# Where the band matmuls of the layer 0 attention get their queries: GpSimd copies, or zero-filled versions in scratch

## The chip, the cores and the metric

The kernel runs on one core of a Trainium2 chip. The core has a matrix engine (TensorE, PE in the profile; its weight loads are listed as PEld), a vector engine (VectorE, DVE), an engine for activations (ScalarE, ACT), a slower general engine (GpSimd, POOL) and a queue from which all transfers of this kernel are issued (SyncE, SP). Every engine works through its own list of instructions in order; an instruction that waits holds up all that stand behind it on that engine. The metric is the device time of one execution in microseconds (us); before the change it is 3945.27 us, the median of three runs (3943.41 to 3945.44).

## What is computed

A network of two layers in the macaron form works on x of 16 batches x 512 tokens x 128 features. Layer 0 is half a feed-forward block with 4-bit block quantization, attention with relative positions, and half a feed-forward block again; layer 1 has two mixture-of-experts blocks with a linear attention between them. The change touches only the attention of layer 0:

```
x = x + 0.5 * _L0_ffn_ref(_layernorm(x), ...)
x = x + _L0_attn_ref(_layernorm(x), ...)          # B=16, S=512, 16 heads of 8
x = x + 0.5 * _L0_ffn_ref(_layernorm(x), ...)
...
dist = jnp.clip(idx[None, :] - idx[:, None], -R, R) + R        # R = 64
pe_k = rel_emb_k[dist]; pe_v = rel_emb_v[dist]
q = q / sqrt(hd)
score = einsum('bhqd,bhkd->bhqk', q, k) + einsum('bhqd,qkd->bhqk', q, pe_k)
attn = softmax(score)
ctx = einsum('bhqk,bhkd->bhqd', attn, v) + einsum('bhqk,qkd->bhqd', attn, pe_v)
```

The second term of the score depends on the distance of query and key only within 64 tokens; outside it is constant per query. So it needs extra matmuls only for tiles near the diagonal, the band.

## The kernel before

**Units of work.** Layer 0 takes the 16 batches one after the other, each in two halves of 256 queries; batch b and half give unit u = 2b + half, 32 units in all. For a unit, `maxima` computes all scores once to find each query's maximum (VectorE, line 324), and `main` computes them a second time, with the negative maximum as an extra row of the contraction, takes exp on ScalarE (line 352) and multiplies by V (lines 361 and 363) and by the relative value table (line 378). Each pass has 32 tiles: 4 blocks of 128 keys by 8 blocks of 32 queries.

**A score tile** (`scores`) is 128 keys x 512 columns (8 values x, 16 heads, 4 residues j). Query 4x+j in the stored order of a block stands for one query; j is called its residue of four. Four matmuls (line 253) of 128 columns give q.k, with queries from `BD`, a tensor that is zero outside its diagonal blocks. If the tile is in the band, eight more matmuls (line 257) of 64 columns add the relative term: the table `ET`, shifted by x, is the stationary operand, and the queries of one x come from `TQ`. The 128 rows of the contraction are four groups of 32 partitions, one per residue; of each 24 rows are used (8 of the high half of the query, 8 of the low half, 8 of the high half again, f16 each). A column of residue j must be zero in the groups of the other residues. There are 8192 matmuls of line 253 and 7168 of line 257.

**How queries get there.** `prep` makes the queries of a batch: a projection on TensorE, a copy to SBUF on ScalarE that sorts them by block, x and j (line 276), the high half on VectorE and the low half on GpSimd (`f16split`, lines 142 and 143). SP writes them to scratch in device memory, QS[16 heads, 29 rows, 512] (line 282), and writes four more rows for the side terms (line 289). `load` reads them back for one half: into `BD` (line 309), and into `TS` (line 310), each residue group receiving all 256 queries. Then four GpSimd copies (line 313), one per residue, take every fourth query from TS and put it into TQ[64 blocks of four, 16 heads, 4 residues], whose other entries were set to zero once in the setup. So the 64 columns of a line 257 matmul lie side by side in TQ. There are three TQ and three BD, used in turn by unit, and one TS.

**Order.** The program is one stream of generators that `interleave` steps through by due times: `main` of unit u, the maxima of the following unit, `prep` of a batch two ahead (in the first 0.7 of an even unit), the feed-forward block of other batches in small steps, and `fin`, the end of the attention. `load` of unit u+1 is issued in the middle of the maxima of unit u. The scheduler then simulates this stream and fixes the order on each engine. All transfers are in the SP queue: the writes of the queries, the loads of BD, TS and KS, the maxima's way through scratch (MD, lines 336 and 338: written, read back into row 28 of BD; `main` needs it), the value part's way (RD, lines 387 and 390), loads and stores of x (lines 456 and 467).

**Other work on VectorE and GpSimd.** The feed-forward block quantizes on both: for a tile of 128 x 704 or 128 x 256, VectorE lines 70 to 78 (74, 76, 77 and 78 read and write SBUF only), then GpSimd lines 79 and 81. The layer norm takes `ln_ve` on VectorE (line 58), a power on GpSimd (line 59) and `ln_mr` on VectorE (line 60).

Of the kernel before, what the change touches and what calls it, by code (L numbers as in the profile page):

```python
# [9 lines left out]
F16 = mybir.dt.float16  # L10
# [130 lines left out]
def f16split(nc, src, hi, lo, eng_lo):  # L141
    nc.vector.tensor_copy(hi,src)
    eng_lo.tensor_tensor(lo,src,hi,ALU.subtract)

class Attn0:

    def __init__(a, s, wk, pp, wqkv, bqkv, wout, bout, rek, rev):
        nc=s.nc; a.s=s; a.nc=nc
        c=s.const; dr=s.dram
# [32 lines left out]
        lo=OFF+24-64  # L182
# [28 lines left out]
            nc.scalar.copy(a.TV[:,:,i*8:i*8+8,:].rearrange("p x v d -> p v x d"),ps.rearrange("p (v x d) -> p v x d",x=8,d=8))  # L211

        a.BD=[c.tile([128,4,4,256],F16,name=f"a0_BD{i}") for i in range(3)]
        a.TQ=[c.tile([128,64,16,4],F16,name=f"a0_TQ{i}") for i in range(3)]
        a.TS=c.tile([128,16,256],F16,name="a0_TS")
        a.KS=[c.tile([128,2,2048],F16,name=f"a0_KS{i}") for i in range(2)]
        a.V=[c.tile([128,4,2,168],F32,name=f"a0_V{i}") for i in range(2)]
        a.cr=[c.tile([128,1024],F32,name=f"a0_cr{i}") for i in range(1)]
# [12 lines left out]
            for sd in range(2): nc.scalar.activation(t[:,sd,:],a.BD[2].rearrange("p g h q -> p (g h q)")[:,0:2048],AF.Identity,bias=rm[:,sd:sd+1])  # L231
        zr=wk.tile([16,512],F16,name="zr"); nc.vector.memset(zr,0.0)
        a.QS=[dr.tile([16,29,512],F16,name=f"QS{i}") for i in range(2)]
        a.KSd=[dr.tile([16,24,512],F16,name=f"KSd{i}") for i in range(2)]
        a.MD=[dr.tile([16,256],F16,name=f"MD{i}") for i in range(2)]
        a.X=4*8*1024+1024
# [10 lines left out]
    def scores(a, out, kt, half, b, BD, TQ, KS):  # L247

        nc=a.nc; blk=half*8+b
        sd=a.side(kt,blk); ib=a.inband(kt,blk)  # L250
        o4=out.rearrange("p (x g c) -> p g x c",x=8,g=4)
        for g in range(4):
            nc.tensor.matmul(o4[:,g],KS[:,sd,g*512+kt*128:g*512+(kt+1)*128],BD[:,g,:,b*32:b*32+32].rearrange("p h (x j) -> p x h j",j=4),start=(g==0),stop=(not ib and g==3),skip_group_check=True)  # L253
        if ib:
            for x in range(8):
                w0=kt*128-blk*32-x+a.OFF
                nc.tensor.matmul(out[:,x*64:x*64+64],a.ET[:,w0:w0+128],TQ[:,b*8+x].rearrange("p h j -> p (h j)"),start=False,stop=(x==7),skip_group_check=True)  # L257

    xnT={}; pend={}; last=None
    def prep(a, b, xb, wk, pM):  # L260
        s=a.s; nc=a.nc
        i=b%2
        QS=a.QS[i]; KSd=a.KSd[i]
        xn=wk.tile([128,4,128],F32,name="xn")
        yield from s.ln_steps(xb,xn,wk,4)
        ps=pM.tile([128,512],F32,name="mps")
        for j in range(4): nc.tensor.transpose(ps[:,j*128:(j+1)*128],xn[:,j,:],a.ident)
        xnT=a.xnT[b]=wk.tile([128,512],F32,name="xnT",bufs=2); nc.scalar.copy(xnT,ps); yield
        for z in range(2):
            ps=pM.tile([128,512],F32,name="mps")  # L270
            nc.tensor.matmul(ps,a.w[:,z*128:(z+1)*128],xnT,start=True,stop=True)
            f=wk.tile([128,512],F32,name="qk0") if z==0 else wk.tile([128,4,128],F32,name="xn").rearrange("p a b -> p (a b)")
            if z==0:
                for hf in range(2):
                    c=slice(hf*256,hf*256+256)
                    nc.scalar.activation(f[:,c].rearrange("p (b x j) -> p b j x",j=4,x=8),ps[:,c].rearrange("p (b j x) -> p b j x",j=4,x=8),AF.Identity,bias=a.bq[:,0:1],scale=float(1/np.sqrt(8.0)))
                q=f
            else: nc.scalar.activation(f,ps,AF.Identity,bias=a.bq[:,1:2])
            hi=wk.tile([128,512],F16,name="qkhi",bufs=2); lo=wk.tile([128,512],F16,name="qklo")
            f16split(nc,f,hi,lo,nc.gpsimd)  # L280
            for p,t in enumerate((hi,lo,hi) if z==0 else (hi,hi,lo)):
                nc.sync.dma_start((QS,KSd)[z][:,p*8:p*8+8,:],t)
            yield
        ps=pM.tile([128,512],F32,name="mps")
        nc.tensor.matmul(ps[:32],a.eb.rearrange("p a b -> p (a b)"),q,start=True,stop=True)
        rhi=wk.tile([128,512],F16,name="qkhi",bufs=2)[:32]; rlo=wk.tile([128,512],F16,name="qklo")[:32]
        nc.vector.tensor_copy(rhi,ps[:32]); nc.vector.tensor_tensor(rlo,ps[:32],rhi,ALU.subtract)
        for sd in range(2):
            nc.sync.dma_start(QS[:,24+2*sd,:],rhi[16*sd:16*sd+16]); nc.sync.dma_start(QS[:,25+2*sd,:],rlo[16*sd:16*sd+16])
        yield  # L290
# [14 lines left out]
    def load(a, b, half):  # L305
        nc=a.nc; i=b%2
        u=(2*b+half)%3; BD=a.BD[u]; TQ=a.TQ[u]; QS=a.QS[i]
        for j in range(4):
            nc.sync.dma_start(BD[j*32:j*32+29,:,j,:],QS.rearrange("(g j) r q -> j r g q",j=4)[j][:,:,half*256:half*256+256])
            nc.sync.dma_start(a.TS[j*32:j*32+24],QS[:,0:24,half*256:half*256+256].rearrange("h r q -> r h q"))  # L310
        for j in range(4):
            p=slice(j*32,j*32+24)
            nc.gpsimd.tensor_copy(TQ[p,:,:,j],a.TS[p,:,j::4].rearrange("p h y -> p y h"))  # L313

    def maxima(a, b, half, wk, pS, pM):

# [121 lines left out]
def layer0(tc, s, w, src, dst, nb=16):  # L438
# [3 lines left out]
    with ExitStack() as c:  # L442
# [51 lines left out]
        def run(g):  # L494
            for _ in g: pass
        run(prep(0)); run(prepV(0)); loads(0); run(mxs(0,0)); loads(1); ffn2(head,1); run(prep(1)); run(part(14)); ffn2(head,2)
        S=[(part(99999),33*2*nb,W['part'],2*nb+W['part'])]
        for b in range(nb):
            for h in range(2):
                u=2*b+h  # L500
                def at(g,n,f,t): S.append((g,n,u+f,u+t))
                at(A.main(b,h,X,wk,big,pS,pA,pM),59,0,1)
                at(A.fin(b,h,X,wk,pM),5,1+W['fin'][0],1+W['fin'][1])
                at(tail(b,h),21,1+W['fin'][1]+.001,1+W['fin'][1]+W['tail'])
                if b+hl<nb: at(head(b+hl,h),21,*W['head'])
                if h==0 and b+pl<nb: at(prep(b+pl),11,*W['prep'])
                if h==1 and b+1<nb: at(prepV(b+1),1,*W['V'])
# [470 lines left out]
```

## Time and profile before

| what | value | from |
|---|---|---|
| median of 3 runs | 3945.27 us | the times |
| the profiled execution | 3944.92 us, of it a span of 3943.2 us | the times, the page |
| score tiles of layer 0 | first reduce at 117.6 us, last exp ends at 2083.5 us | rows of lines 324 and 352 |
| busy in 32 stretches of 61 us from 150 us on, mean | PE 53.98, DVE 46.24, ACT 29.24, POOL 21.33 us | busy time by stretch |
| DVE in two neighbouring stretches (943 to 1004, 1004 to 1065) | 53.05 and 42.30 us | the same |
| granted clock of TensorE in most of these stretches | 0.94 | the same |

Times in a row of the timeline are the start, from the start of the span, and the duration. A group's row in the page gives its count, its busy time, the mean duration of one, and how long the engine sat idle just ahead of it and who ended that. Matmuls are pipelined, so the rate of a matmul is read from the starts of neighbouring rows and not from its duration. Some 125 us pass from one batch to the next: the writes of the queries begin at 828.1, 952.3 and 1077.8 us.

### The profile page before, as it was taken

To read this page: it belongs to the slowest core of one execution; us is meant where nothing else is said; L and a number is where in the kernel's file an instruction comes from. 1 tells how busy PE (TensorE), PEld (TensorE's weight loads), DVE (VectorE), ACT (ScalarE), POOL (GpSimd) and SP (SyncE) were. 2 spreads that over 40 slices of the span, in tenths; PEclk is the share of its full clock that TensorE was granted. 3 is DMA by queue.
4 is the path that set the end of the run, shared out by engine and by line. 5 is a ranking of instruction groups with operands and counts; after the bars stand their busy time and mean duration, and the time that the engine had idled before them with its cause. 6 is when DMAs were issued, how large, how long until landed. Compare 5 with 4: busy or idle time off the path is not lost.

```text
span 3943.2 us, 98508 instructions
## 1 busy us (share of the span) xinstructions
PE 2997.4 (76%) x41613; PEld 2162.8 (55%) x41613; DVE 2588.3 (66%) x6567; ACT 1711.1 (43%) x3389; POOL 1100.2 (28%) x883
## 2 busy tenths in 40 slices
PE   4788898988889889899985577770688888888540
PEld 2566677676777667767763344430465555555320
DVE  5768777887778777887754366664546556555375
ACT  2245445444444445445442344531445445444321
POOL 4443433334233333433312011103311111010214
PEclk7799999999999999999996777875899899888665
DMA  1221222122121221112101100003321122111114
GB/s 51 48 53 40 55 44 50 42 47 54 43 48 35 56 50 40 49 39 56 40 19 45 42 25 33 30 22 88 92 71 53 48 68 65 44 52 29 58 33 122
DMA packets 263248, 194.88 MB, mean 49 GB/s; under 512 B 74428, under 2 KB 228886, under 8 KB 262679
## 3 DMA queue, kind: packets, MB, share of 16 engines
q1 hardware_dynamic: 262806, 188.59, 18.6%
q8 instruction: 327, 5.36, 0.6%
q14 instruction: 115, 0.93, 0.1%
HBM read 111.57 MB, written 76.92 MB: 48 GB/s over the span
## 4 chain that ended last, share of the span: by engine, by line
PE 42%; DVE 20%; DMA 10%; ACT 7%; POOL 2%; issue 2%; SPq 1%; DVEq 0%; POOLq 0%; ACTq 0%
PE sps L253 8%; PE mps L685 5%; PE sps L257 3%; DVE mx L324 3%; PE av L361 2%; PE pp L849 2%; PE rps L378 2%; DMA d_m<-FMD 2%; ACT f_PT L644 2%; PE av L363 1%; PE mps L649 1%; PE mps L138 1%; DVE moe L687 1%; DVE cx L403 1%; DMA X<-d_x 1%
## 5 line engine op out<-in xcount | busy, mean ns | idle before, releaser
L253 PE MATMUL sps<-a_BD,a_KS 128*128 128x128 f16 x8192 | 763.4, 225 | 162.6 <-DVE mx L324 117.4
L324 DVE TRANSPOSE_TENSOR_REDUCE mx<-sps 128x16 f32<-128x512 f32 x1024 | 708.3, 705 | 242.5 <-PE sps L253 140.0
L352 ACT ACTIVATE PT<-sps 128x512 f32<-128x512 f32 x1024 | 579.3, 597 | 512.6 <-PE sps L257 269.9
L253 PEld LDWEIGHTS <-a_KS 128*128 128x128 f16 x8192 | 548.9, 100 | 317.6 <-issue 267.1
L687 DVE SCALAR_TENSOR_TENSOR moe<-mps,oh,moe 128x128 f32<-128x128 f32 x1024 | 331.0, 345 | 240.6 <-PE mps L685 224.6
L79 POOL TENSOR_TENSOR q_M<-q_y,q_M 128x256 f32<-128x256 f32 (+2 forms) x135 | 158.1, 1172 | 795.2 <-DVE q_y L78 508.4
L59 POOL TENSOR_TENSOR ln_rs<-ln_ve,negh 128x4 f32<-128x4 f32 (+1 forms) x192 | 175.4, 922 | 720.2 <-DVE ln_ve L58 651.9
L257 PE MATMUL sps<-a_TQ,a_ET 128*128 128x64 f16 x7168 | 371.7, 195 | 3.2 <-POOL a_TQ L313 3.2
L313 POOL COPY a_TQ<-a_TS 24x1024 f16<-24x1024 f16 x128 | 330.4, 2581 | 93.8 <-PE sps L257 47.3
L257 PEld LDWEIGHTS <-a_ET 128*128 128x128 f16 x7168 | 311.0, 100 | 14.0 <-issue 12.2
L685 PE MATMUL mps<-f_W,T 128*128 128x512 f32 x512 | 288.1, 680 | 2.6 <-DVE moe L687 2.0
L361 PE MATMUL av<-PT,a_V 128*32 128x256 f32 (+2 forms) x3584 | 264.0, 346 | 0.0
L851 DVE TENSOR_TENSOR a_at<-pp,a_cm 128x1024 f32<-128x1024 f32 x128 | 154.5, 1219 | 90.3 <-PE pp L849 89.8
L378 PE MATMUL rps<-PT,a_TV 128*32 128x64 f32 x7168 | 212.3, 230 | 0.8 <-issue 0.6
L849 PE MATMUL pp<-a_F 64*128 64x128 f32 x2048 | 174.0, 309 | 17.5 <-DVE a_at L851 11.0
L849 PEld LDWEIGHTS pp<-a_F 64*128 64x128 f32 x2048 | 146.2, 209 | 63.8 <-issue 28.5
L378 PEld LDWEIGHTS rps<-PT,a_TV 128*32 128x32 f32 x7168 | 137.7, 112 | 60.4 <-issue 27.8
L649 PE MATMUL mps<-f_PT,v 128*32 128x128 f32 x1024 | 55.7, 388 | 149.8 <-ACT f_PT L644 149.8
L361 PEld LDWEIGHTS av<-PT,a_V 128*32 128x32 f32 x3584 | 130.5, 109 | 53.9 <-issue 15.1
L831 ACT ACTIVATE a_F<-pp 128x1024 f32<-128x1024 f32 x128 | 127.8, 1025 | 63.6 <-PE pp L829 54.8
L62 ACT ACTIVATE d_m<-d_m,ln_mr,ln_rs 128x128 f32<-128x128 f32 x128 | 52.2, 483 | 229.0 <-DVE ln_mr L60 173.9
L685 PEld LDWEIGHTS mps<-f_W,T 128*128 128x128 f32 x512 | 98.3, 214 | 90.6 <-issue 64.6
(320 smaller groups left out, 5657.1 us busy)
## 6 DMA issues: line engine op xcount, KB each, us to landing
a_TS<-QS SPq DMA_DIRECT2D x128, 192.0 KB
RD<-RV SPq DMA_DIRECT2D x32, 512.0 KB
a_KS<-KSd SPq DMA_DIRECT2D x128, 96.0 KB
a_QK<-a1d SPq DMA_DIRECT2D x128, 96.0 KB
xn<-X SPq DMA_DIRECT2D x32, 256.0 KB
YD<-xn SPq DMA_DIRECT2D x32, 256.0 KB
FMD<-moe SPq DMA_DIRECT2D x32, 256.0 KB
d_x<-X SPq DMA_DIRECT2D x32, 256.0 KB
```

The source lines that it names most:

```text
L59: nc.gpsimd.tensor_tensor(rs,ve,s.negh[:,:n],ALU.pow); yield
L79: nc.gpsimd.tensor_tensor(M[:P],y[:P],M[:P],ALU.subtract)
L253: nc.tensor.matmul(o4[:,g],KS[:,sd,g*512+kt*128:g*512+(kt+1)*128],BD[:,g,:,b*32:b*32+32].rearrange("p h (x j) -> p x h j",j=4),start=(g==0 ...
L257: nc.tensor.matmul(out[:,x*64:x*64+64],a.ET[:,w0:w0+128],TQ[:,b*8+x].rearrange("p h j -> p (h j)"),start=False,stop=(x==7),skip_group_chec ...
L313: nc.gpsimd.tensor_copy(TQ[p,:,:,j],a.TS[p,:,j::4].rearrange("p h y -> p y h"))
L324: r=nc.vector.tensor_reduce(mx[:,kt,:,bb],ps.rearrange("p (i c) -> p i c",c=32),axis=AX.X,op=ALU.max,apply_transpose=True)
L352: nc.scalar.activation(pt[:,:,bb*32:bb*32+32].rearrange("p h (x j) -> p x h j",j=4),ps.rearrange("p (x h j) -> p x h j",x=8,j=4),AF.Exp)
L361: nc.tensor.matmul(o[:,0:q3],V[:,kt,0,h*9:h*9+32],pt[:,h,0:q3],start=fs,stop=(kt==3),skip_group_check=True,tile_position=(0,cg*32))
L378: nc.tensor.matmul(rps[cg*32:cg*32+32,col:col+64],a.TV[:,x,v0:v0+4,:].rearrange("p v d -> p (v d)"), PT[k][:,:,bb*32+4*x:bb*32+4*x+4], sta ...
L685: nc.tensor.matmul(ps,yT[:,j*128:(j+1)*128],a.W[:,e2*4:e2*4+4,:],start=True,stop=True)
L687: nc.vector.scalar_tensor_tensor(moe[:,j,:],ps[:,e*128:(e+1)*128],oh[:,j,e2*4+e:e2*4+e+1],moe[:,j,:],ALU.mult,ALU.add)
L849: nc.tensor.matmul(ps[:,hh,bs],f[hh*64:hh*64+64,1,bs],f[hh*64:hh*64+64,0,bs],start=True,stop=True)
```

## The change

TS and the GpSimd copies go. In `prep`, after the split, the high half is copied once more by VectorE and the low half once more by GpSimd, into `HM`, two tiles of [128, 4, 512] that were set to zero in the setup: position [j, n] receives query n if n has residue j, and stays zero otherwise. SP writes each of the four versions to a new scratch tensor QM[4 residues, 16 heads, 24 rows, 512], three times (rows 0 to 7 high, 8 to 15 low, 16 to 23 high): 12 writes per batch of 128 partitions x 1 KB. In `load`, residue group j of TQ is filled straight from QM[j] by a transfer of the shape that TS had. TQ is now [128, 16 heads, 256 queries], and a line 257 matmul reads its 64 columns as 16 runs of 4 queries, one run per head.

```
-        a.TQ=[c.tile([128,64,16,4],F16,name=f"a0_TQ{i}") for i in range(3)]
-        a.TS=c.tile([128,16,256],F16,name="a0_TS")
+        a.TQ=[c.tile([128,16,256],F16,name=f"a0_TQ{i}") for i in range(3)]
+        a.HM=[c.tile([128,4,512],F16,name=f"a0_HM{i}") for i in range(2)]
+        for t in a.HM: nc.gpsimd.memset(t,0.0)
...
+        a.QM=[dr.tile([4,16,24,512],F16,name=f"QM{i}") for i in range(2)]
...
-                nc.tensor.matmul(out[:,x*64:x*64+64],a.ET[:,w0:w0+128],TQ[:,b*8+x].rearrange("p h j -> p (h j)"),start=False,stop=(x==7),skip_group_check=True)
+                nc.tensor.matmul(out[:,x*64:x*64+64],a.ET[:,w0:w0+128],TQ[:,:,b*32+4*x:b*32+4*x+4],start=False,stop=(x==7),skip_group_check=True)
...
             f16split(nc,f,hi,lo,nc.gpsimd)
+            if z==0:
+                for t,e,m in ((hi,nc.vector,a.HM[0]),(lo,nc.gpsimd,a.HM[1])):
+                    e.tensor_copy(bass.AP(tensor=m.tensor,offset=m.offset,ap=[m.ap[0],[513,4],[4,128]]),t.rearrange("p (y j) -> p j y",j=4))
+                for p,t in enumerate((a.HM[0],a.HM[1],a.HM[0])):
+                    for j in range(4): nc.sync.dma_start(a.QM[i][j][:,p*8:p*8+8,:],t[:,j,:])
...
-            nc.sync.dma_start(a.TS[j*32:j*32+24],QS[:,0:24,half*256:half*256+256].rearrange("h r q -> r h q"))
-        for j in range(4):
-            p=slice(j*32,j*32+24)
-            nc.gpsimd.tensor_copy(TQ[p,:,:,j],a.TS[p,:,j::4].rearrange("p h y -> p y h"))
+            nc.sync.dma_start(TQ[j*32:j*32+24],a.QM[i][j][:,:,half*256:half*256+256].rearrange("h r q -> r h q"))
```

## The prediction

> **What bounds the kernel now.** I read the page first. The copies that the change removes are the largest single item of POOL, and nobody seems to wait for them: the matmuls that use TQ sat idle before them only 3.2 us.
>
> ```profile
> L253 PE MATMUL sps<-a_BD,a_KS 128*128 128x128 f16 x8192 | 763.4, 225 | 162.6 <-DVE mx L324 117.4
> ...
> L257 PE MATMUL sps<-a_TQ,a_ET 128*128 128x64 f16 x7168 | 371.7, 195 | 3.2 <-POOL a_TQ L313 3.2
> L313 POOL COPY a_TQ<-a_TS 24x1024 f16<-24x1024 f16 x128 | 330.4, 2581 | 93.8 <-PE sps L257 47.3
> ```
>
> PE's largest idle item is VectorE (mx L324). So I looked at VectorE while the copies run. POOL's timeline, then VectorE's (start, us, then the operation):
>
> ```profile
> 958.01 10.85 POOL L313 COPY a_TQ<-a_TS 24x1024 f16<-24x1024 f16 x4 [0.34 <-PE sps L257]
> ```
>
> ```profile
> 959.42 1.61 DVE L74 TENSOR_TENSOR q_y<-f_h,hq_ri 128x704 f32<-128x704 f32 x1
> ...
> 962.16 1.60 DVE L76 TENSOR_SCALAR q_M<-q_y 128x704 uint32<-128x704 uint32 x1
> ...
> 964.28 2.23 DVE L77 TENSOR_SCALAR q_M<-q_M 128x704 f32<-128x704 f32 x1
> 966.42 0.51 DVE L125 SCALAR_TENSOR_TENSOR f_h<-mps,f_h 128x352 f32<-128x352 f32 x1
> ...
> 967.48 1.86 DVE L78 SCALAR_TENSOR_TENSOR q_y<-q_y,q_M 128x704 f32<-128x704 f32 x1
> ...
> 973.84 0.89 DVE L74 TENSOR_TENSOR q_y<-f_h,hq_ri 128x704 f32<-128x704 f32 x1
> ...
> 976.00 0.48 DVE L76 TENSOR_SCALAR q_M<-q_y 128x704 uint32<-128x704 uint32 x1
> ...
> 977.37 0.49 DVE L77 TENSOR_SCALAR q_M<-q_M 128x704 f32<-128x704 f32 x1
> ...
> 978.78 0.86 DVE L78 SCALAR_TENSOR_TENSOR q_y<-q_y,q_M 128x704 f32<-128x704 f32 x1
> ```
>
> The same four operations take 1.61, 1.60, 2.23 and 1.86 us beside a copy, and 0.89, 0.48, 0.49 and 0.86 us 14 us later without one: 4.6 us lost in one batch. L125, which reads PSUM, keeps its length. VectorE has no gap from 955 to 980, and PE starves there:
>
> ```profile
> 966.99 0.33 PE L418 MATMUL mps<-ident,cn 128*128 128x128 f32 x1 [1.35 <-DVE f_h L125]
> 967.61 0.39 PE L253 MATMUL sps<-a_BD,a_KS 128*128 128x128 f16 x4 [0.29 <-DVE mx L324]
> ...
> 970.03 0.58 PE L253 MATMUL sps<-a_BD,a_KS 128*128 128x128 f16 x4 [0.76 <-DVE mx L324]
> ```
>
> In the busy time by stretch, PE has 1.94 us of the 5 from 965 to 970, and from 968.2 on it is granted half its clock for 6.8 us. So layer 0 is bound by PE and VectorE in turn, and here the copies hold up VectorE.
>
> **Removed: the stretching.** For each VectorE instruction that overlapped a copy I took its duration less the median of its form without a copy. 71 instructions lose over 0.3 us each, 92.6 us together: 13.1 us from 90 to 330, 13.1 us from 330 to 586, 65.1 us from 586 to 1840, 1.2 us behind. Mostly they are lines 77, 78, 76, 74 in the odd units and L58 in the even ones (2.35 us at 1163.24 against 0.16). The chain of waits is listed from 589 us on; of the 65.1 us, 57.2 lie in its pieces: 88%. I take this share for 330 to 1840 too and nothing for the start: 0.88 x 78.2 = 68.8 us gained. From below nothing (VectorE catches up anyway), from above all 92.6. PE can follow: per batch it sits idle 13.7 us (gaps in its timeline, mean of seven batches), 4.0 of them 10 to 20 us after the query writes, where the stretched instructions are; the 5.7 us at 80 to 85 us wait for a load of x and stay.
>
> **Added on VectorE:** 16 copies of 512 f16 elements, over strides. Nearest rows: the cast L142 of as many elements, 0.42 us; L287 from PSUM, 0.66 us. I take 0.55 us: 8.8 us, at 88% on the path 7.7 (bounds 6 and 11).
>
> **Added on POOL:** 16 copies of 512 elements. L313 takes 2.58 us for 1024, so 1.29; L143, also 512, takes 1.16. I take 1.2 us, 20 us in all, against 330.4 removed. They stretch VectorE as the old ones did: 92.6/330.4 = 0.28 us per us, so 5.4 us, on the path 4.7 (bounds 0 and 20). POOL's later work moves forward.
>
> **PE.** The line 257 matmuls now read runs of 4 queries. Line 253 reads such runs already, from BD. Starts of neighbouring rows:
>
> ```profile
> 1002.37 0.63 PE L253 MATMUL sps<-a_BD,a_KS 128*128 128x128 f16 x8
> 1002.83 0.39 PE L257 MATMUL sps<-a_TQ,a_ET 128*128 128x64 f16 x8
> 1003.06 0.39 PE L253 MATMUL sps<-a_BD,a_KS 128*128 128x128 f16 x4
> ```
>
> Eight of line 253 take 0.46 us, 57.5 ns for 128 columns; eight of line 257 take 0.23 us, 28.8 ns for 64: 0.45 ns per column in both. So I cost this at nothing. [...]
>
> **SP and the transfers.** Removed are 128 loads of TS, added 128 of TQ of equal size. Added are 12 writes per batch of 128 x 1 KB, like QS<-qkhi (median 0.584 us to issue, longest 1.286): 12 x 0.584 = 7.0 us per batch. The first four wait for VectorE's copy of the high half, four for POOL's copy of the low half. Behind them in SP stand the rest of the query writes and, in the changed order, MD, the maxima that the next `main` needs:
>
> ```profile
> 952.26 1.22 SPq L282 DMA_DIRECT2D QS<-qkhi  x2
> ...
> 954.79 1.28 SPq L336 DMA_DIRECT2D MD<-mn  x2
> ...
> 961.08 2.45 SPq L338 DMA_DIRECT2D a_BD<-MD  x4
> ```
>
> MD is issued at 954.79 now; in the new order it stands behind the 12 writes and the side rows of line 289, whose high half VectorE finishes at 962.2, so at about 963.6. The read back starts 6.3 us after it, takes 2.45 us to issue and some 2 to land: 974.5. The first matmul that needs it starts at 979.9, or 975.3 if 4.6 us are gained ahead of it. So it is hidden, by under 1 us; if that cover is gone, each us costs 14 us (14 batches). Even units have no query writes: there MD keeps its place (the gap from the read back's issue to the matmul is 15 to 17 us now). RD and the next BD load move back as much and are needed later (BD issued at 978.6 for tiles from 1019.4 on). TQ's load must wait for the last line 257 matmul of the unit three back (957.9 in this batch), as the copy does now. The 25 MB more ride on engines that are busy two tenths.
>
> **Setup.** Two more zero fills on POOL, half of 3.5 us each, with 1.7 us of idle time behind them; the first loads of TQ stand behind 7 us of writes instead of behind a copy of 2.5 us. I take 3 us (bounds 0 and 6).
>
> **Sum**, against the profiled execution: 3944.9 - 68.8 + 7.7 + 4.7 + 3.0 = 3891.5 us. The median of the runs shown is 0.3 us above that execution. I predict 3891 us.
>
> **Rivals.**
> 1. *More than the sum.* The PE gap at 965 is also what the half clock follows. Without the gap, 6.8 us at half clock become 3.4 us of PE work gained per batch, so 4.0 + 3.4 = 7.4 us: 14 x 7.4 = 104 us less 15.4 for the added parts, about 3856 us. For it: the slow period follows that gap in every batch. Against: VectorE is the fuller engine from 955 to 985 (30 us; PE has 25 busy). [...]
> 2. *Nothing is left.* VectorE gains, but runs into the load of x (5.7 us of PE idle per batch) or an MD about 4 us late takes back the 4 us per batch: 53/14 = 3.8. 3935 to 3953 us.
> 3. *Slower: MD comes late.* If the 12 writes issue at the longest time of such a row, 1.286 us, MD's row comes 8.4 us later, 7.6 us after it is needed: 14 x 7.6 = 106 us, 3891 + 106 = 3997 us. It decides from 3.8 us of lateness on, which is 0.97 us per write. For it: the BD loads in this queue do take 2.29 us each. Against: those have 464 pieces of 512 bytes; these have 128, as QS, which stayed at 0.58.
> 4. *Slower: the short runs cost PE.* If a line 257 matmul took twice its time, 7168 x 28.8 ns = 206 us, about 4097 us. The rate of line 253 speaks against it.
>
> **How the numbers follow.** The forecast's own case (3865 to 3925) 0.60; rival 1 0.14; rival 2 0.11; rival 3 0.12; rival 4 0.03. A difference under 0.2%, 7.9 us, can't be told from none; that is 3937 to 3953. Rival 2 gives 0.07 of its chance to it and 0.04 to faster, so faster 0.78, same 0.07, slower 0.15. The range leaves out most of the slower cases and the far end of rival 1: 3846 to 3953. The forecast's own range is 3865 to 3925.
>
> **What would show it.** In the profile after: L74, L76, L77 and L78 with one duration each (0.89, 0.48, 0.49, 0.86 us), apart from those beside other POOL work; the idle time of L253 behind mx L324 well below 117.4 us; eight line 257 matmuls still in 0.23 us; writes of QM near 0.58 us; no wait of L253 for a_BD<-MD. A wait of several us there, once per batch, would prove rival 3; the slow clock gone in the odd units, rival 1. The prediction is wrong if VectorE's durations fall and the time does not.

## The result

The kernel after takes 3902.89 us (median of 4 runs, 3902.23 to 3912.94), the kernel before 3944.34 us beside it (4 runs, 3943.23 to 3945.44). The ratio is 0.9907, 95% interval 0.9886 to 0.9928: 41.5 us, or 0.9%, faster. The prediction said 3891 us, 3865 to 3925 for its own case.

Lines of the kernel after that answer to those shown of before (the two groups of score matmuls are now L255 and L259; the columns are busy us, mean ns of one, and the idle time before them with what ended most of it; the row of L255 is from the list of groups, which names more than one waker):

```profile
span 3900.5 us, 98555 instructions
...
PE 2979.8 (76%) x41613; PEld 2145.0 (55%) x41613; DVE 2529.4 (65%) x6583; ACT 1706.0 (44%) x3389; POOL 804.4 (21%) x773
...
L255 PE MATMUL sps<-a_BD,a_KS 128*128 128x128 f16 x8192 | 752.1, 221 | 130.0 <-DVE mx L328 57.1 <-ACT PT L356 26.8 <-DVE ln_ve L58 25.9
...
L259 PE MATMUL sps<-a_TQ,a_ET 128*128 128x64 f16 x7168 | 364.6, 194 | 0.0
```

The copies are gone from POOL (1100.2 to 804.4 us). VectorE is busy 58.9 us less, with 16 more instructions. L255 waits 57.1 us behind the maxima instead of 117.4, but 25.9 us more, in six waits, are now put down to L58, which stands beside the maxima in VectorE's queue: in the odd batches this is the gap behind the load of x that was counted under the maxima before. All its idle time fell from 162.6 to 130.0 us. The band matmuls, which now read runs of four queries, take 194 ns on the mean against 195.

The answers for lines 76, 77 and 78 from 586 to 1840 us (duration in ns: shortest, median, longest), first of before:

```profile
L76 DVE TENSOR_SCALAR q_M<-q_y x80: 247/476/1619, 589.2 to 1823.5; 128x704 uint32<-128x704 uint32 x41, 128x256 uint32<-128x256 uint32 x39
L77 DVE TENSOR_SCALAR q_M<-q_M x80: 273/478/2234, 591.3 to 1825.1; 128x704 f32<-128x704 f32 x41, 128x256 f32<-128x256 f32 x39
L78 DVE SCALAR_TENSOR_TENSOR q_y<-q_y,q_M x80: 382/853/1893, 594.5 to 1826.9; 128x704 f32<-128x704 f32 x41, 128x256 f32<-128x256 f32 x39
```

and of after:

```profile
L76 DVE TENSOR_SCALAR q_M<-q_y x80: 248/480/749, 590.8 to 1813.5; 128x256 uint32<-128x256 uint32 x40, 128x704 uint32<-128x704 uint32 x40
L77 DVE TENSOR_SCALAR q_M<-q_M x80: 246/483/753, 591.7 to 1814.0; 128x256 f32<-128x256 f32 x40, 128x704 f32<-128x704 f32 x40
L78 DVE SCALAR_TENSOR_TENSOR q_y<-q_y,q_M x80: 380/639/893, 593.0 to 1815.1; 128x256 f32<-128x256 f32 x40, 128x704 f32<-128x704 f32 x40
```

The third number is what to look at: the longest of each fell from 1.6 to 2.2 us to 0.75 to 0.89 us. (The medians mix the two widths and say little.) L74, the fourth of these lines, still takes up to 1.80 us, in one case beside GpSimd's L81.

Where the 42.7 us between the two spans came from is seen by cutting each span where the first exponential of layer 0 starts and where the last one ends. Before, these stand at 161.73 and 2083.54 us, after at 171.46 and 2034.93. So the start lost 9.7 us, the sixteen batches between gained 58.3 us (1921.8 to 1863.5), and the rest, nearly all layer 1, lost 5.9 us (1859.63 to 1865.57) though none of its code was touched.

Each batch, from its first exponential to that of the next, in us, for nine of the kernels here (the last column is what follows the last exponential; worked out from the traces):

```
                     first exp  batches 0 to 15                                                 rest
before                  162  130 133 125 124 125 124 126 125 124 125 124 125 122 105 102 83   1859.6
after                   171  123 121 121 123 119 124 121 124 118 122 120 125 113 108  99 83   1865.6
e4_start                169  121 122 121 121 121 125 116 126 119 120 118 124 116 108  99 82   1867.5
e7_writes_twice         175  134 134 127 127 126 126 126 124 126 128 127 126 120 113  99 84   1872.1
e8_six_x                170  122 118 123 125 124 123 124 122 124 124 121 124 119 109 103 83   1875.6
e9_copies_in_place      174  129 129 129 130 129 128 128 128 129 130 129 130 123 106  99 82   1861.9
e10_twice_two_lo        177  135 131 118 127 120 126 116 124 119 127 121 127 115 113  99 83   1880.3
e11_two_lo              170  123 122 120 121 118 126 119 125 118 122 117 125 113 107 100 83   1869.0
e12_six_x_lo            170  126 117 123 120 121 120 120 121 120 120 119 121 117 107 103 82   1875.6
```

In the kernel after, batches 4 to 11 alternate between some 120 and 124 us. They take 121.7 us on the mean, 3.1 less than before: per batch, PE's idle time fell from 13.7 to 11.6 us, and its busy time, which grows where the granted clock drops, from 111.1 to 110.1. (At half clock, matmuls of line 253 in the kernel before started 107 ns apart, at full clock 57, both medians. The granted clock from 586 to 1840 us is 0.95 before and 0.97 after.)

The timeline (start us, us, and in brackets the idle time before) shows a wait that the kernel before had only once from 300 to 1840 us, of 0.8 us. SyncE's queue of the kernel after in batch 6:

```profile
924.71 8.90 SPq L287 DMA_DIRECT2D QM<-a_HM  x12
933.66 0.60 SPq L289 DMA_DIRECT2D QS<-qklo  x1
934.35 1.20 SPq L289 DMA_DIRECT2D KSd<-qkhi  x2
938.24 0.52 SPq L289 DMA_DIRECT2D KSd<-qklo  x1
938.86 2.53 SPq L296 DMA_DIRECT2D QS<-qkhi  x2
941.48 1.29 SPq L340 DMA_DIRECT2D MD<-mn  x2
...
943.49 0.36 SPq L296 DMA_DIRECT2D QS<-qklo  x1
...
950.26 0.44 SPq L296 DMA_DIRECT2D QS<-qklo  x1
```

POOL's in the same stretch:

```profile
922.72 1.16 POOL L143 TENSOR_TENSOR qklo<-qk,qkhi 128x512 f16<-128x512 f32 x1 [12.27 <-DVE qkhi L142]
923.95 1.81 POOL L285 COPY a_HM<-qklo 128x512 f16<-128x512 f16 x1
936.22 1.99 POOL L143 TENSOR_TENSOR qklo<-xn,qkhi 128x512 f16<-128x512 f32 x1 [10.46 <-DVE qkhi L294]
```

VectorE's, and PE's right behind it:

```profile
942.30 0.68 DVE L294 TENSOR_TENSOR qklo<-mps,qkhi 32x512 f16<-32x512 f32 x1 [3.18 <-DMA KSd<-qklo]
```

```profile
943.65 0.39 PE L255 MATMUL sps<-a_BD,a_KS 128*128 128x128 f16 x4 [1.20 <-DVE mx L328]
```

The tile qklo has one buffer, and three instructions of a batch write it in turn. The low half of the queries must leave it by QS<-qklo, which now stands behind the twelve writes of QM and is issued at 933.66. Only then can POOL write the low half of the keys (936.22), whose own transfer is issued at 938.24, and only when that has left can VectorE write the side rows' low half: it sits still for 3.18 us, and PE behind it for 1.20. The prediction did not look at this buffer.

### The profile page after: what moved, and what is told of

The parts are those of the page before. It is cut to its first block, busy times and chain, and to the rows that moved or that the text cites. A ratio compares the mean times of both kernels' runs of the same rounds, so it can differ in the third digit from the quotient of the medians.

```text
span 3900.5 us, 98555 instructions
## 1 busy us (share of the span) xinstructions
PE 2979.8 (76%) x41613; PEld 2145.0 (55%) x41613; DVE 2529.4 (65%) x6583; ACT 1706.0 (44%) x3389; POOL 804.4 (21%) x773
## 4 chain that ended last, share of the span: by engine, by line
PE 48%; DVE 21%; DMA 12%; ACT 8%; issue 4%; POOL 3%; SPq 3%; DVEq 0%; POOLq 0%; ACTq 0%
PE sps L255 8%; PE mps L689 5%; DVE mx L328 4%; PE sps L259 4%; PE av L365 3%; PE rps L382 3%; PE pp L853 2%; DMA d_m<-FMD 2%; PE mps L120 2%; ACT f_PT L648 2%; PE mps L138 2%; PE av L367 2%; DVE moe L691 1%; PE mps L653 1%; DMA MD<-mn 1%
## 5 line engine op out<-in xcount | busy, mean ns | idle before, releaser
L255 PE MATMUL sps<-a_BD,a_KS 128*128 128x128 f16 x8192 | 752.1, 221 | 130.0 <-DVE mx L328 57.1
L255 PEld LDWEIGHTS <-a_KS 128*128 128x128 f16 x8192 | 534.2, 98 | 303.5 <-issue 249.3
L59 POOL TENSOR_TENSOR ln_rs<-ln_ve,negh 128x4 f32<-128x4 f32 (+1 forms) x192 | 174.7, 919 | 927.1 <-DVE ln_ve L58 835.7
L259 PE MATMUL sps<-a_TQ,a_ET 128*128 128x64 f16 x7168 | 364.6, 194 | 0.0
L79 POOL TENSOR_TENSOR q_M<-q_y,q_M 128x256 f32<-128x256 f32 (+2 forms) x135 | 158.5, 1178 | 884.2 <-DVE q_y L78 556.0
L259 PEld LDWEIGHTS <-a_ET 128*128 128x128 f16 x7168 | 305.4, 98 | 0.0
L365 PE MATMUL av<-PT,a_V 128*32 128x256 f32 (+2 forms) x3584 | 255.2, 350 | 0.0
L62 ACT ACTIVATE xn<-xn,ln_mr,ln_rs 128x128 f32<-128x128 f32 x256 | 103.7, 482 | 67.1 <-DVE ln_mr L60 66.6
```

The costliest lines, as they stand in the source:

```text
L59: nc.gpsimd.tensor_tensor(rs,ve,s.negh[:,:n],ALU.pow); yield
L62: nc.scalar.activation(out[:,j,:],xb[:,j,:],AF.Identity,bias=mr[:,j:j+1],scale=rs[:,j:j+1])
L79: nc.gpsimd.tensor_tensor(M[:P],y[:P],M[:P],ALU.subtract)
L365: nc.tensor.matmul(o[:,0:q3],V[:,kt,0,h*9:h*9+32],pt[:,h,0:q3],start=fs,stop=(kt==3),skip_group_check=True,tile_position=(0,cg*32))
```

## The experiments

The kernels were timed in three groups, each beside runs of the kernel before, whose medians were 3938.5, 3955.0 and 3953.2 us; so ratios are compared, against 0.9907 of the kernel after.

**1. The copies back, over the new query tiles.** In the kernel after, behind the loads of TQ:

```diff
+        for j in range(4):
+            v=TQ[j*32:j*32+24,:,j::4].rearrange("p h y -> p y h")
+            nc.gpsimd.tensor_copy(v,v)
```

> The changed kernel with four GpSimd copies per half put back into load: each copies TQ's own residue group onto itself (24 x 1024 f16, every fourth query, as before), so no value changes. The way of the queries stays the new one. Theory 1 (the gain is VectorE work that the copies stretched): L74, L76, L77 and L78 on 128x704 again take 1.6 to 2.2 us beside a copy, first to last exp of layer 0 goes from 1863.4 us back to about 1920, the time to about 3903 + 57 = 3960 us. Theory 2 (the gain is a shorter wait for TQ or another order of work): first to last exp stays within 10 us of 1863, the time within 10 us of 3903.

Measured: 4221.54 us, ratio 1.0709 (1.0681 to 1.0737). Group line of the copies on its page:

```profile
L320 POOL COPY a_TQ<-a_TQ 24x1024 f16<-24x1024 f16 x128 | 616.1, 4813 | 280.2 <-DMA a_TQ<-QM 247.2
```

Both times expected were missed, since two things changed at once. A copy with 512 bytes between neighbours on both sides takes 4.81 us, where the old one, with 8 bytes between neighbours on the side it wrote, took 2.58; and POOL now waits 247.2 us for loads of TQ, with LayerNorm's and the quantizer's work behind it in its queue: from 300 to 1840 us PE's waits for the quantizer's L81 came to 62.3 us, against 0.2 before. VectorE's L74, L76, L77 and L78 beside such a copy took 3.77, 4.70, 4.14 and 4.15 us, where the batch that the prediction shows has 1.61 to 2.23 beside copies of 2.7: the longer copy stretched them more.

**2. Fills in the place of the copies.** As before, but writing only:

```diff
+        for j in range(4):
+            v=TQ[j*32:j*32+24]
+            nc.gpsimd.memset(bass.AP(tensor=v.tensor,offset=v.offset+j+1,ap=[v.ap[0],[4,1023],[1,3]]),0.0)
```

> The changed kernel with four GpSimd zero fills per half in load, about as long as the copies (24 x 3069 f16, some 2.6 us), on entries of TQ that are zero anyway: GpSimd writes SBUF but reads nothing. Theory 1a (any GpSimd instruction on SBUF holds up such VectorE work): as with the copies back, L74, L76, L77, L78 all at 1.6 to 2.2 us and about 3960 us. Theory 1b (what they share differs for reads and writes): L76 and L77, one input each, stretched; L74 and L78, two inputs from SBUF, at 0.89 and 0.86 us; lines 77, 58, 76 and 71 had 62.5 of the 89.7 us, so about 3903 + 0.7 x 57 = 3943 us. Theory 2 (no sharing): 3903 us.

Measured: 4141.41 us, ratio 1.0509 (1.0482 to 1.0537). The same wait spoils it (the fills wait 307.2 us for loads), so the time decides nothing. The durations say more. Where nothing but fills of 2.7 us ran on GpSimd, L76 on 256 columns took 1.96 us at the median (11 cases) and L58, on two columns, 1.40 (24 cases); of nine L76 on 704 columns eight kept 0.47 to 0.48 us, seven of which had begun before the fill or within 0.07 us of its start. L74 and L78 of 704 columns kept their 0.82 to 0.89 us (10 of 10); the eight L78 that also met L79, which reads two tensors, took 1.58 to 1.59.

**3. The copies of the kernel before, on ScalarE.**

```diff
-            nc.gpsimd.tensor_copy(TQ[p,:,:,j],a.TS[p,:,j::4].rearrange("p h y -> p y h"))
+            nc.scalar.copy(TQ[p,:,:,j],a.TS[p,:,j::4].rearrange("p h y -> p y h"))
```

> The kernel before, with the four copies per half on ScalarE in place of GpSimd; TS, QS and TQ as they were, nothing written to QM. Theory 1: the stretched durations go as in the changed kernel, ScalarE gets 128 copies of about 1.1 us (140 us, in stretches where it is busy 29 of 61 us), and there is no later start: 3944 - 57 = 3887 us, up to 3905 if ScalarE's copies hold up exps. Theory 2 (the gain needs queries that come ready from scratch): 3944 us or more.

Measured: 4020.03 us, ratio 1.0190 (1.0154 to 1.0226). What the copies stretched is back: L76 and L78 of 704 columns take at most 0.52 and 0.88 us from 300 to 1840 us. VectorE's work beside GpSimd's other lines, 79 and 81 above all, is still held, by 62 us in the first 2150 us, as in the kernel after (63 us). But a copy takes ScalarE 2.52 us, 322 us in all, and not the 1.1 us expected (ScalarE's activations of 128x1024 elements in layer 1 take 1.03). PE now waits for ScalarE instead (73.9 us for cn, 44.2 for hT from 300 to 1840 us). A batch took 127.1 us. Taking the stretch away is not worth such a price on an engine that PE waits for.

**4. The start.** In the kernel after, the zero fills of HM go from the setup into the first batch's `prep`, and that batch's writes of QM onto ScalarE's queue:

```diff
-        for t in a.HM: nc.gpsimd.memset(t,0.0)
...
+                if b==0:
+                    for t in a.HM: nc.gpsimd.memset(t,0.0)
...
-                    for j in range(4): nc.sync.dma_start(a.QM[i][j][:,p*8:p*8+8,:],t[:,j,:])
+                    for j in range(4): (nc.scalar if b==0 else nc.sync).dma_start(a.QM[i][j][:,p*8:p*8+8,:],t[:,j,:])
```

> The changed kernel with a shorter start: the zero fills of HM stand in front of their first use, and the 12 writes of the first batch to QM are issued from ScalarE's queue. In the changed kernel the first maximum is taken at 127.6 us against 117.6 before. Theory 1 (SP's 7.7 us of writes and the 2.9 us of fills are that loss): first maximum at 118 to 120 us, the time 3903 - 8 = 3895 us. Theory 2 (something else is late at the start): 127 us, 3903 us. The order of layer 1 differs a little in each of these kernels; from the last exp of layer 0 to the end it took 1859.7 us before and 1865.6 us after.

Measured: 3895.39 us, ratio 0.9882 (0.9854 to 0.9911). The first maximum came at 123.2 us (before 117.6, after 127.6), the first exponential at 169.2 (161.7 and 171.5). So of the 10 us that the first maximum lost, 4.4 went to these two causes; of the first exponential's 9.7, 2.2.

**5 and 6. GpSimd work that nobody waits for.** In the kernel after, four copies of 24 x 896 elements per half from a constant table into a spare tile (run 5), or twelve zero fills of it (run 6):

```diff
+            nc.gpsimd.tensor_copy(a.DD[p],a.ET[p,0:364].rearrange("p (a c) -> p a c",c=4)[:,0:64,0:1].to_broadcast([24,64,14]))
```

```diff
+            for _ in range(3): nc.gpsimd.memset(a.DD[j*32:j*32+24],0.0)
```

> The kernel after, plus four GpSimd copies per half (24 partitions x 896 elements each, strided source) from a constant table into a spare tile that nobody reads: they add work and wait for nothing and nobody waits for them, unlike the first run, whose copies wrote the query tiles. The output is the reference's. Theory 1 (what the removed copies cost was that VectorE's work beside them stretched): L74, L76, L77 and L78 (704 columns) take 1.6 to 2.3 us beside a copy against 0.88, 0.48, 0.52 and 0.85; at about 2.2 us a copy, 282 us in all and 0.28 us lost per us of copy, 79 us are lost, 88% of it on the path: some 70 us, about 3970 us, nearly all between the first and the last exponential (1863 to about 1930 us). If only the share of the time holds that the kernel before lost in steady batches (3 us per batch), 3945 us. Theory 2 (the gain came from the removed wait and the moved order, not from the stretching): durations as in the kernel after, 3895 to 3910 us.

> The kernel after, plus twelve GpSimd zero fills per half (24 x 896 each) of the same spare tile, which write and read nothing and wait for nothing. The output is the reference's. Theory 1a (any GpSimd work in SBUF holds VectorE): all of L58, L76, L77, L74 and L78 stretch, at the share of the run before this one per us of fill: 384 fills of 0.6 to 0.9 us, 230 to 350 us, 60 to 95 us lost, 3955 to 3985 us. Theory 1b (only VectorE's operations with one input from SBUF are held, as the second run suggested where the fills also waited for loads): L76, L77 and L58 stretch, L74 and L78 keep 0.88 and 0.85 us; about half of that, 3925 to 3945 us. Theory 2: nothing stretches, 3895 to 3910 us.

Measured: 4018.47 us, ratio 1.0165 (1.0151 to 1.0178), and 3991.32 us, ratio 1.0089 (1.0076 to 1.0102). Neither is what it was made to be, as POOL's row of run 5 shows (tenths of 40 slices of the span):

```profile
POOL 8532222122222222221111111103311111010214
```

With no data to wait for, the added instructions were laid down by the scheduler as early as POOL had room: POOL is busy eight tenths of the first slice, and five and three of the next two (four, two and two in the kernel after). They held up the setup, and the first maximum came at 188.7 us (189.5 in run 6) instead of 127.6. From batch 4 to 11 a batch took 122.4 and 122.1 us, but all of the added instructions stood before batch 4, so neither time decides between the theories. The durations of run 6 agree with run 2: beside nothing but fills of 0.86 us, L76 and L77 of 704 columns took 0.63 and 0.89 us at the median (0.49 and 0.52 alone) and L71, on 44 columns, 0.47 (0.15 alone), while all 18 of L74 and L78 of 704 columns that met fills alone kept 0.84 to 0.89.

**7. Each write of QM twice.**

```diff
-                    for j in range(4): nc.sync.dma_start(a.QM[i][j][:,p*8:p*8+8,:],t[:,j,:])
+                    for j in range(8): nc.sync.dma_start(a.QM[i][j%4][:,p*8:p*8+8,:],t[:,j%4,:])
```

> The kernel after, with each of the twelve writes of QM issued twice, the same data: 12 more in SP's queue, 7.0 us per batch (12 x 0.584), ahead of the rest of the query writes and of MD. The output is the reference's. As the prediction had it, MD's cover was under 1 us: 6 us late per batch and 14 batches, some 85 us, about 3988 us, with a wait of L255 for a_BD<-MD of about 6 us per batch in the trace. As the trace after is read (read back of MD issued 9.5 to 13.2 us ahead of the matmul that needs it in odd units, some 2 of that to land), all of it is hidden: under 0.5 us per batch, 3900 to 3912 us, plus up to 7 us at the start, where the first load of TQ stands behind the writes.

Measured: 3997.58 us, ratio 1.0103 (1.0088 to 1.0119), 0.0196 above the kernel after: some 77 us. That is near the number of the first theory, and yet not its mechanism: from 300 to 1840 us there is no wait for a_BD<-MD, and in the odd units the last issue of that read back still ends 8.7 to 9.6 us ahead of the first matmul that needs it (batches 4 to 11). The waits of VectorE, and of PE, from 300 to 1840 us (us in total, times, longest):

```profile
DVE qklo L294 <- DMA KSd<-qklo: 55.2, 12, 5.6
```

```profile
PE mps L132 <- DVE qklo L294: 29.2, 11, 4.3
```

The wait that the kernel after has in two of these batches (7.0 us) is now in twelve, at 4.6 us each.

**8. Six buffers for x.** PE's longest gap in a steady batch of before, 5.6 us, waits for VectorE, which waits for a load of x into a buffer that is still being stored. From run 4's kernel:

```diff
-        xk=c.enter_context(tc.tile_pool(name="xk",bufs=5))
+        xk=c.enter_context(tc.tile_pool(name="xk",bufs=6))
...
-        mk=wk.tile([128,2,8,8],F32,name="mk")
+        mk=wk.tile([128,2,128],F32,name="cn")[:,0].rearrange("p (s b x) -> p s b x",s=2,b=8)
```

> The fourth run's kernel (zero fills of HM within the first batch's preparation, its QM writes on ScalarE's queue) with six buffers for x instead of five, so that the load of the next batch need not wait for the store of the oldest; the maxima's small tile shares the buffer of cn to make room. The output is the reference's. If VectorE's wait for that load (L55 behind x, 41 us in the chain's middle part, 52 us over the stage, and PE's idleness behind it) lies on the path: 35 to 50 us less than the fourth run's 3895, about 3850 us. If VectorE and PE only wait elsewhere instead (they are full just after): 3885 to 3900 us.

Measured: 3935.10 us, ratio 0.9949 (0.9936 to 0.9963): slower than run 4. The wait for x is gone, but VectorE's waits from 300 to 1840 us have in third place:

```profile
DVE qklo L295 <- DMA KSd<-qklo: 59.2, 12, 6.0
```

It is the wait of run 7, with single writes: once the feed-forward half starts earlier, this buffer is what is late. The edit also lets the maxima's small tile share the buffer of cn, and PE's waits ahead of that tile's transpose, from 300 to 1840 us, grew from 13.3 us in run 4 to 30.4; what the sharing costs by itself no run separates.

**9. Copies in the old place.** In the kernel after, four copies per batch from HM into a spare tile, tied by a tiny copy behind the second L143, so that they stand where the odd units' copies stood:

```diff
+        D=a.DD; m=a.HM[1]; nc.gpsimd.tensor_copy(D[:,0,0],lo[:,0:4])
+        for j in range(4):
+            p=slice(j*32,j*32+24); d=D[p]; t=m[p]
+            nc.gpsimd.tensor_copy(bass.AP(tensor=d.tensor,offset=d.offset,ap=[d.ap[0],[1,4],[64,14],[4,16]]),bass.AP(tensor=t.tensor,offset=t.offset+j,ap=[t.ap[0],[16,4],[4,14],[128,16]]))
```

> The kernel after, plus four GpSimd copies per batch (24 partitions x 896 elements, strided on both sides) from the zero-filled tile of the low half into a spare tile that nobody reads; a tiny copy ties them behind the second L143, so that they stand where the old copies of the odd units stood, and no other engine waits for them. The output is the reference's. At the old rate a copy takes 2.2 us, 145 us in all with 64 of them. Theory 1 (the old copies cost by stretching VectorE's work): the instructions beside them are stretched as before, L74, L76, L77 and L78 to 1.6 to 2.2 us; 0.28 us per us of copy is 41 us lost, up to 58 us if they fall on the same four lines as in the kernel before; 88% of it on the path: 36 to 51 us, 3939 to 3954 us, or a ratio to the kernel before of 0.998 to 1.004. Theory 2 (the gain came from a shorter POOL queue or from the order): POOL's q_M L79 stands behind them as it did behind the old copies, so the same time is lost but the durations on VectorE stay at 0.88, 0.48, 0.52 and 0.85. Theory 3 (the gain came from elsewhere): 3900 to 3910 us, whatever the durations.

Measured: 4001.09 us, ratio 1.0115 (1.0102 to 1.0128), 0.0208 above the kernel after, some 82 us. POOL's timeline in one batch:

```profile
1239.47 9.38 POOL L297 COPY a_DD<-a_HM 24x896 f16<-24x896 f16 x4
```

VectorE's beside it and after it:

```profile
1245.88 0.92 DVE L77 TENSOR_SCALAR q_M<-q_M 128x704 f32<-128x704 f32 x1
...
1246.88 2.01 DVE L71 TENSOR_SCALAR hq_sc<-hq_sc 128x44 f32<-128x44 f32 x1
...
1249.20 0.84 DVE L78 SCALAR_TENSOR_TENSOR q_y<-q_y,q_M 128x704 f32<-128x704 f32 x1
...
1256.40 0.48 DVE L77 TENSOR_SCALAR q_M<-q_M 128x704 f32<-128x704 f32 x1
```

and PE's (the added lines move L255 to L256 and the maxima to L333):

```profile
1249.32 0.59 PE L256 MATMUL sps<-a_BD,a_KS 128*128 128x128 f16 x4 [2.57 <-DVE mx L333]
```

L71 works on 44 columns, 0.15 us elsewhere. Here it takes 2.01 us and ends at 1248.89, when the last copy ends (1239.47 + 9.38 = 1248.85); PE then has sat idle for 2.57 us behind the maxima. Counted as in the prediction, 46 of VectorE's instructions lost over 0.3 us beside a copy, 79.5 us together. Beside GpSimd's work of every kind, in the first 2150 us, it was 150 instructions and 163.5 us, against 80 and 63.0 in the kernel after: 100.5 us more. From the first exponential to the last the kernel took 93.4 us more (1956.9 against 1863.5). Theory 1's mechanism, then, with a price twice as high as expected: 64 copies of 2.36 us are 150.8 us, and cost 0.53 us per us of copy, not 0.28; that all of them stand where VectorE has little idle time may be why, but no run moves them. Theories 2 and 3 fall: durations changed, and the time with them, and nobody waits for GpSimd's queue (from 300 to 1840 us VectorE waited 2.6 us and PE 0.2 us for GpSimd in the kernel before, and neither did in this run). Per batch 7.1 us were lost, 4.6 of PE's idle time and 2.4 of its busy time, with a granted clock of 0.95 against 0.97 from 586 to 1840 us.

**10 to 12. The buffer of qklo.** Run 10 is run 7 with two buffers for qklo, run 11 is run 4 with two. In run 12, which is run 8 otherwise, the side rows' low half goes into the buffer of xn, since six buffers of x leave no room:

```diff
-            hi=wk.tile([128,512],F16,name="qkhi",bufs=2); lo=wk.tile([128,512],F16,name="qklo")
+            hi=wk.tile([128,512],F16,name="qkhi",bufs=2); lo=wk.tile([128,512],F16,name="qklo",bufs=2)
```

```diff
-rlo=wk.tile([128,512],F16,name="qklo")[:32]
+rlo=wk.tile([128,4,128],F32,name="xn").rearrange("p a b -> p (a b)")[:32,0:256].bitcast(F16)
```

> The seventh run's kernel (each write of QM issued twice) with two buffers instead of one for the low half, qklo. The output is the reference's. Theory 1 (the writes do their harm through the one buffer of qklo: L294 on VectorE must wait until KSd<-qklo has left, 55 us in twelve waits): VectorE's wait for KSd<-qklo is gone, the steady batches return from 126.2 to about 122 us, and the time to 3910 to 3935 us, ratio 0.991 to 0.996 (8 us at the start stay). Theory 2 (the queue itself is late: MD, or the loads behind it): still 3975 to 4000 us, ratio 1.005 to 1.012, with the wait moved to a_BD<-MD or to the load of x.

> The fourth run's kernel (start mended) with two buffers for qklo. The output is the reference's. Theory 1 (the single writes already cost through that buffer, POOL's L143 waiting 86 us for QS<-qklo and VectorE's L294 7 us for KSd<-qklo): VectorE's 7 us and what follows POOL's delay come back, 0.5 to 2 us per batch, 3870 to 3890 us, ratio 0.982 to 0.987. Theory 2 (at single writes the wait is off the path): as the fourth run, ratio 0.986 to 0.990.

> The eighth run's kernel (six buffers for x) in which the low half of the side rows, rlo, no longer shares the one buffer of qklo but lies in the buffer of xn. The output is the reference's. Theory 1 (what the eighth run won at the load of x, its wait gone, it lost at L294's wait for KSd<-qklo, 59 us in twelve waits): that wait is gone, 4 to 5 us per batch less than its 123.2, 3865 to 3885 us, ratio 0.979 to 0.984. Theory 2 (the loss came with another order of the work, the even units 10 us longer): 3910 to 3940 us, ratio 0.990 to 0.997.

Run 10: 3946.60 us, ratio 0.9989 (0.9975 to 1.0003), a miss between the two theories. The wait for KSd<-qklo is gone and the steady batches are back at 122.4 us, as theory 1 had it; 45 of run 7's 77 us come back. Some 32 do not: in the profiled execution, which is itself 12 us above the median, the first two batches take 22 us more than in the kernel after, the other batches 14, the start 5, and layer 1, which nothing in the edit touches, 15. Part of that is the queue again: L294 now waits for transfers that stand further ahead, those of the queries, and PE behind it for 29.9 us; two of these waits, near 353 and 1823 us, are of some 10 us each (VectorE's waits from 300 to 1840 us):

```profile
DVE qklo L294 <- DMA QS<-qklo: 19.7, 7, 9.1
...
DVE qkhi L294 <- DMA QS<-qkhi: 10.2, 2, 9.9
```

Run 11: 3898.78 us, ratio 0.9868 (0.9852 to 0.9884). It lies where both expectations allow it, and the steady batches (121.0 us against 121.2 in run 4) hardly moved, so for single writes the wait is next to free with five buffers of x.

Run 12: 3894.87 us, ratio 0.9850 (0.9838 to 0.9863). Against run 8 that is 0.0099 less, 39 us, in the direction of theory 1 and just short of its range. Of the wait, part is left, now for POOL's second L143, which still waits for QS<-qklo (VectorE's waits from 300 to 1840 us):

```profile
DVE xn L295 <- POOL qklo L143: 26.8, 12, 5.0
```

Its steady batches take 120.2 us and no longer alternate. Its interval lies wholly under that of the kernel after: of the kernels here it has the lowest ratio, though run 11's interval overlaps it.

## Why the prediction was right, and where it was off

**The cause.** Right, and shown from both sides. With the copies gone, or on ScalarE (run 3), what VectorE's instructions lose beside GpSimd's work falls from 142.0 us (144 instructions, first 2150 us) to 63.0 and 62.1 us; with new copies in the old place (run 9) it is 163.5 us, 100.5 more than in the kernel after, and the time between the first and the last exponential grows by 93.4. The sign that the prediction set, one duration each for L74, L76, L77 and L78, came out for the most part: the 63 us that are left stand beside GpSimd's other work, lines 79 and 81 above all.

**The size of the gain.** The sum had 68.8 - 7.7 - 4.7 = 56.4 us for layer 0's batches; they gained 58.3. But it lies elsewhere than the prediction put it. Of the 65.1 us lost after 586 us it took 88% as gain, 57 us over ten batches, less 0.9 each for the added copies: 4.8 us per batch. The steady batches, 4 to 11, gave 3.1. The first three batches gave 7, 12 and 4 us, twice the 11.5 that the sum had for 330 to 586 us, where it set the stretch before 330 us at nothing, and batch 12 gave 9. Two errors of opposite sign met, so that the total of the batches came out within 2 us was luck. In the steady batches part of PE's gain went into new gaps: in batches 5, 7, 9 and 11, PE sits idle for 1.5 us ahead of the transpose of mk and for 1.7 to 2.0 us ahead of that of cx. They are not the qklo wait's, for with that out of the way (run 11) the batches still alternate; with six buffers of x (run 12) they no longer do.

**The added copies** were priced too low: VectorE's takes 1.02 us at the median, not 0.55, some 7.5 us more in all, and POOL's 1.76, not 1.2. Beside POOL's, VectorE's instructions lost 2.8 us, less than the 5.4 of the sum. No run takes these copies out by themselves.

**PE** read the runs of four queries at no cost, as the prediction said: 194 ns each against 195, 364.6 us in all against 371.7. That such a matmul could take twice its time was rival 4's assumption, and no run shows it: rival 4 is out.

**SyncE's queue and MD.** The price of a write was right (0.602 us at the median against 0.584), the step behind it wrong. The prediction had MD "hidden, by under 1 us"; in the odd units of batches 4 to 11 the last issue of the read back ends 9.5 to 13.7 us ahead of the matmul (15.7 to 17.5 before), and where the chain of before lists one of its transfers, that takes 1.71 us (at 712.89) and 1.73 us (at 1337.29). It put MD behind all the side rows' writes; in the queue shown above, MD is issued at 941.48, and two of these writes, QS<-qklo, come after it. Its reason why the writes would not be slow was a misreading: 464 pieces of 512 bytes are four loads of BD, and one load, of 58 KB, has 116, fewer than the 128 of a write. That such a load took 2.29 us at the median to issue was no price of its own either, as it took 0.78 in the kernel after. Rival 3's lateness was real, its place was not: what the queue makes late first is the one buffer of qklo. Run 7 shows this buffer's wait, run 10 takes it away and leaves shorter ones for the transfers ahead of it, and MD was in time in both.

**Setup.** Predicted 3 us (0 to 6), measured 9.7 at the first exponential. Run 4 shows that the fills and the first writes explain 4.4 of the 10 us at the first maximum; the rest was not settled.

**Layer 1.** The sum had nothing for it, and it took 5.9 us more. In all twelve kernels of the experiments its code is that of before, and what follows the last exponential took 1861.6 to 1880.3 us against 1859.6. Of the 5.9 us, half is PE's busy time (1208.8 to 1211.8 us) and half its idle time (650.8 to 653.7); in run 10 all of the 20.6 us more than before are idle time (672.0). The order of its instructions shifts a little with each edit of layer 0; whether this order is the cause stays open, the more so as each figure is from one execution, and executions of one kernel lie up to 22.5 us apart (run 10). It is also what keeps run 12, with the shortest batches, from a larger gain: 1875.6.

**Rival 1** came about in part. In the steady batches the time at half clock fell from 13.7 to 7.7 us per batch, but PE's busy time by 1.1 us only, where the prediction's rate, half of that time, gives 3.0 and its own case had 3.4; why it is so little was not settled. **Rival 2**'s load of x did not grow into the gain: the gap that waits for it shrank from 5.6 to between 2.6 and 4.6 us in the steady batches.

So 3902.9 stands 12 us above the forecast, and 11 of them are these: 6.7 us of start and 5.9 of layer 1 too little in the sum, and batches 1.9 us better than it.

## What to carry to other kernels

An engine's work that nobody waited for was on the path here, through what it did to another engine's durations (L77 took 2.23 us beside a copy and 0.49 apart from it): compare the same instruction form beside it and apart from it before calling it free. When writes are put into a queue, look first at what frees single buffers behind them in that queue, and only then at the value that some later stage needs; doubling the writes shows which of them is near. An added instruction without data to wait for is no probe of a place, as the scheduler laid it down wherever there was room (runs 5 and 6): tie it to data of that place.

## What the hardware showed beyond this

- VectorE's instructions beside a GpSimd copy look held rather than slowed. In the kernel before, 71 of them lost over 0.3 us; between the tenth and the ninetieth percentile they ended 0.03 to 0.50 us after the end of a copy. Small ones were held as long as large ones: L58, on two columns, went from 0.17 to 2.4 us at the longest, L78, on 704, from 0.86 to 2.5.
- Which of them were held differed with what GpSimd did. Beside copies, forms with two inputs in SBUF (L74, L78) and forms with one (L76, L77, L71, L58) were held; beside zero fills the second kind only: 28 of 28 of L74 and L78 (704 columns) that met fills alone in runs 2 and 6 kept their length, and all ten that also met L79, L81 or L143, which read whole tiles, did not (1.5 to 2.4 us); one that met L59, which reads two to four columns, kept 0.89.
- What a GpSimd copy of 24 partitions took differed with its strides: 1024 elements took 2.58 us when written 8 bytes apart and 4.81 us when written 512 bytes apart; 896 elements took 2.36 us strided on both sides and 0.95 us written densely from repeated elements.
- The granted clock went with how busy PE had been just before, and no long gap was needed. In batches 4 to 11, cut into stretches of 3.41 us (the half clock came in periods of one, two or three of these; in the kernel before each lasted 6.83 us), each of the 54 falls to half clock in the kernels before and after and in runs 9 and 12 came behind a stretch in which PE was busy 0.51 of the time or less; of the 1007 stretches at full clock that no fall followed, all but two (0.48 and 0.49) had 0.52 or more. In the kernel before, once in every steady batch, the longest gap ahead of a fall was 1.35 us, with smaller ones around it.
